# A two-layer graph attention network on one core: layer 2's destination factors as broadcast rows on ScalarE, and a new place and pace for layer 1's early pairs

## The chip, the core and the metric

The kernel runs on one core of a Trainium2 chip. The metric is the device time of one execution in microseconds; below a run means one execution. The core has five engines with a queue of instructions each: TensorE (PE, with its weight loads as PEld), VectorE (DVE), ScalarE (ACT), GpSimd (POOL) and SyncE (SP), and 16 DMA engines that move data between HBM and the on-chip memory. An engine takes its instructions in order: one that waits holds up all behind it.

## What is computed

6250 nodes with 768 features, 100,000 edges sorted by destination. The features are normalised and rectified, go through two layers of graph attention (four heads of 64 columns, then one head of 256), each followed by a relu, then through two dense layers, and the input is added. Cut to what matters here:

```python
def gat_conv(x, src, dst, W, a_src, a_dst, bias, heads):
    h = (x @ W).reshape(n, heads, -1)
    alpha_s = (h * a_src[None]).sum(-1)
    alpha_d = (h * a_dst[None]).sum(-1)
    e = jax.nn.leaky_relu(alpha_s[src] + alpha_d[dst], 0.2)
    e = jnp.exp(e - segment_max(e, dst)[dst])
    alpha = e / (segment_sum(e, dst)[dst] + 1e-16)
    return segment_sum(h[src] * alpha[:, :, None], dst).reshape(n, -1) + bias
h = jnp.maximum(_layernorm(x), 0.0)
h = relu(gat_conv(h, ..., W1, a_src1, a_dst1, b1, 4))     # layer 1
h = relu(gat_conv(h, ..., W2, a_src2, a_dst2, b2, 1))     # layer 2
return x + (relu(h @ Wm1 + bm1) @ Wm2 + bm2)
```

Every node also has an edge to itself. Numerator and denominator are summed together: a column of ones beside h makes the denominator. The weight of an edge is needed only up to a factor that depends on its destination, since that cancels. With s the source's score and d the destination's, exp(leaky_relu(s + d)) divided by exp(d) is max(exp(s), exp(0.2 s) * rho) with rho = exp(-0.8 d). So a source row carries e1 = exp(s) and e2 = exp(0.2 s), and only rho has to come from the destination. The same weight is exp(s + relu(-0.8 s - 0.8 d)).

## The kernel before

**Feature phase (to about 172 us).** For each of NT = 49 tiles of 128 nodes, x is loaded, normalised and multiplied by W1 (features1, L440); the row of a node, features and powers of its scores, stays on the chip (`kept`) and is stored to a table in HBM (store1, L473).

**Edges.** 782 edge tiles of 128 edges. Two tiles are a pair, four a group g (196 groups), eight a unit u (98), sixteen belong to one step of a node tile t, on average (49). For every edge tile GpSimd issues one indirect DMA (L645), which gathers the 128 source rows from the layer's table into half of a buffer G, one of 20 that hold a pair each. Gathers are issued AHEAD = 8 groups before their use. A buffer comes free when TensorE (and, in layer 1, VectorE) is done with its pair.

**rho to the edges.** For each unit a mask of 0 and 1 in bf16 (node by edge, 128x1024, make_mask L653, VectorE L662) is made in layer 1 and stored to `mask_d` (L664); layer 2 loads it back (fetch_mask L612). meet(t) (L683) multiplies each edge tile's mask with a narrow matrix `win` that holds rho in three bf16 parts: 16 matmuls for a node tile, 12 columns in layer 1 and 3 in layer 2 (L691). join(t) (L694) adds the three parts. `win` is built by prepare (L557), once for each layer.

**A pair (L703).** VectorE makes v = e2 * rho (L712) and w = max(v, e1) (L722 in layer 1, L715 in layer 2). Layer 1 then multiplies the gathered rows by w (L724), and TensorE sums them into the unit's 128 destinations with a one-hot matrix `hot` (L673) as weights. In layer 2 VectorE makes a one-hot matrix that is scaled by w (two L719 for a pair), which is TensorE's weights, and the gathered rows go through as they are. Both are L736 (o_ps), two matmuls and two weight loads for a tile.

**Node steps.** take_sum (L747) adds a unit's sum to the running one (VectorE L753) and copies finished quarters out (ScalarE L762). In layer 1, Node1.steps (L945) divides, transposes, multiplies by W2 and stores the row of table 2 (L966 and after). In layer 2, Node2.steps (L1055): divide (o, L1066), transpose (L912), relu with bias (rT, L918), first dense layer (L1075, then mT by L1080), second (y, bias L1024 and L1085), add x (L1089), store. The tables STEPS_AT and UP_AT give the half-groups at which the steps of a node tile are put into the queues of layer 2.

**Early tiles.** The first gathers of a layer would wait for its whole table. Eleven edge tiles of layer 2 are gathered while its last rows are missing, and the missing rows are added by one-hot matmuls (first_rows L322, first_whole L294). Layer 1 does so for 23 *early pairs* (SOON), which lie eight groups apart from group 11 on. They are gathered in the feature phase from as much of the table as is there (soon_rows L346), stored to `soon_d` in HBM (soon_away L356), loaded back into a buffer when their turn comes (soon_back L362), and completed: soon_sources loads their source numbers, soon_hits (VectorE L379) makes one-hot matrices for the node tiles that were missing, soon_missing (TensorE L389, 1028 matmuls in all) fetches the rows from `kept`, and soon_whole (VectorE L396) adds them. soon_away stores a pair as soon as the table is SOON_HELD = 6 tiles past the pair's stage, and all that are left at the start of layer 1.

**Order.** From L400 on the order on every engine is the order of the program. The loop over groups is:

```python
for g in range(NG):                       # t, j = divmod(g, 4)
    gather(g + AHEAD)
    pair(g, 0)
    advance(g); gather_up(...); make_hot(g + 1)
    if j == 0:   fetch_rows, soon_sources, prefetch(t), meet(t + 1), soon_hits(t)
    elif j == 2: ahead(t), soon_missing(t)
    elif j % 2:  soon_whole(t - 1) where j == 1; make_mask((g + 7) // 2)
    pair(g, 1)
    advance(g, 1)
    if j == 3: join(t + 1)
```

with the soon_ steps in layer 1 only (their number is the early tile k = 2 i + 0 or 1).

## Time and profile before

| | us |
|---|---|
| runs shown, median of 3 | 2571.82 (2562.27 to 2574.3) |
| the profiled execution, own time | 2580.24 |
| its span, first to last instruction | 2578.4 |
| gathers of layer 1 on GpSimd | about 172 to 1340 |
| GpSimd still, end of layer 1 | 1340.4 to 1375.8 |
| gathers of layer 2 | 1375.8 to 2527 |
| mean granted TensorE clock | 0.802 |

A matmul in single precision is two passes in the records, so a tile's L736 appears as two matmuls and two weight loads. The costliest groups of the page after the gathers, with line, engine, operation, operands and count, then busy time and mean duration in ns, and the idle time of the engine ahead of them with what ended most of it:

```profile
L736 PE MATMUL o_ps<-G,hw 128*128 128x258 f32 x1564 | 524.6, 463 | 225.5 <-issue 196.2
L736 PE MATMUL o_ps<-hw,hot 128*128 128x260 f32 x1564 | 504.6, 463 | 207.6 <-issue 128.8
...
L719 DVE TENSOR_SCALAR hw<-iota_ps,dcol,w 128x128 f32<-128x128 f32 x782 | 285.0, 406 | 15.4 <-DVE w L715 0.6
L724 DVE TENSOR_TENSOR hw<-G,e_ps 128x520 f32<-128x520 f32 x391 | 271.8, 695 | 22.5 <-DVE e_ps L722 6.3
L389 PE MATMUL missing<-kept,soon_hit 128*128 128x268 f32 x1028 | 251.4, 398 | 35.2 <-issue 35.2
L379 DVE TENSOR_TENSOR soon_hit<-soon_of,iota_ps 128x1408 f32<-128x1408 int32 (+18 forms) x46 | 75.6, 1643 | 323.2 <-remote 258.8
...
L691 PE MATMUL e_ps<-win,mask 128*128 128x12 bf16 (+1 forms) x1564 | 72.0, 168 | 130.9 <-issue 122.6
```

"issue" is time in which the engine waited for nothing that the profile shows, "remote" a releaser that it could not name. The page's 40 slices show the DMA engines full in the first three (351, 358 and 329 GB/s of the feature phase) and about half busy after. Idle time of an engine that is not the limit costs nothing.

### The profile page before, as it was taken

What the parts mean: (1) busy time and instruction counts of PE and PEld (TensorE: products, weight loads), DVE (VectorE), ACT (ScalarE), POOL (GpSimd) and SP (SyncE); (2) the same over time, 40 slices, a digit from 0 to 9 for tenths busy, and PEclk for the clock granted to TensorE, in tenths of its full rate; (3) what the DMA queues carried; (4) which work ended last, traced back from release to release, by engine and by line L of the source; (5) the groups of instructions that cost most, each with busy time, mean ns of one, the idle gap of its engine ahead of it and who ended that gap; (6) DMA issues with size and microseconds to landing.
All of it is one profiled execution on the core that took longest, in us unless ns stands there. A gap on an engine that the chain in (4) does not pass through costs nothing.

```text
span 2578.4 us, 26497 instructions
## 1 busy us (share of the span) xinstructions
PE 1809.2 (70%) x7727; PEld 1288.6 (50%) x7729; DVE 1397.1 (54%) x4195; ACT 409.4 (16%) x1273; POOL 1523.6 (59%) x1666
## 2 busy tenths in 40 slices
PE   9944768867767777677675656676766766777677
PEld 7732546646545555555553434454444444454455
DVE  7733666666666676576565443444444444444444
ACT  6730011111111111111111011111111111111111
POOL 5366555565655655565554566666666666666661
PEclk9975878878878888887888768777778778877778
DMA  9994444545544544454434434445554555444442
GB/s 351 358 329 114 143 140 137 147 137 147 149 141 143 154 143 143 143 149 138 142 107 125 126 113 152 146 140 152 153 150 136 151 152 156 151 136 145 148 147 76
DMA packets 167328, 400.37 MB, mean 155 GB/s; under 512 B 36631, under 2 KB 54254, under 8 KB 167174
## 3 DMA queue, kind: packets, MB, share of 16 engines
q0 software_dynamic: 75072, 211.10, 29.9%
q1 hardware_dynamic: 90732, 185.99, 21.0%
q10 hardware_dynamic: 1370, 1.48, 0.2%
q8 instruction: 65, 1.06, 0.2%
q14 instruction: 89, 0.73, 0.1%
HBM read 333.87 MB, written 64.56 MB: 155 GB/s over the span
## 4 chain that ended last, share of the span: by engine, by line
PE 30%; issue 22%; DVE 21%; another core or an unknown queue 16%; POOL 4%; DMA 3%; ACT 1%; SPq 0%; DVEq 0%; POOLq 0%; ACTq 0%
PE o_ps L736 17%; PE y_ps L1085 4%; DVE hw L724 4%; POOL G L645 4%; DVE hot L673 4%; PE missing L389 3%; PE h_ps L447 3%; DVE e_ps L722 2%; DVE e_ps L712 2%; DVE hw L719 2%; DMA G<-table,src_i 2%; DVE acc L753 2%; DVE mask L662 1%; PE tp L1075 1%
## 5 line engine op out<-in xcount | busy, mean ns | idle before, releaser
L645 POOL DMA_INDIRECT G<-table,src_i x1507 | 1431.5, 950 | 874.1 <-issue 377.3
L736 PE MATMUL o_ps<-G,hw 128*128 128x258 f32 x1564 | 524.6, 463 | 225.5 <-issue 196.2
L736 PE MATMUL o_ps<-hw,hot 128*128 128x260 f32 x1564 | 504.6, 463 | 207.6 <-issue 128.8
L736 PEld LDWEIGHTS o_ps<-G,hw 128*128 128x128 f32 x1564 | 353.0, 232 | 368.8 <-issue 272.0
L736 PEld LDWEIGHTS o_ps<-hw,hot 128*128 128x128 f32 x1564 | 337.8, 227 | 347.2 <-issue 169.0
L762 ACT ACTIVATE sum<-acc 32x260 f32<-32x260 f32 (+1 forms) x384 | 160.0, 417 | 1421.8 <-DVE hw L724 631.8
L719 DVE TENSOR_SCALAR hw<-iota_ps,dcol,w 128x128 f32<-128x128 f32 x782 | 285.0, 406 | 15.4 <-DVE w L715 0.6
L724 DVE TENSOR_TENSOR hw<-G,e_ps 128x520 f32<-128x520 f32 x391 | 271.8, 695 | 22.5 <-DVE e_ps L722 6.3
L389 PE MATMUL missing<-kept,soon_hit 128*128 128x268 f32 x1028 | 251.4, 398 | 35.2 <-issue 35.2
L379 DVE TENSOR_TENSOR soon_hit<-soon_of,iota_ps 128x1408 f32<-128x1408 int32 (+18 forms) x46 | 75.6, 1643 | 323.2 <-remote 258.8
L389 PEld LDWEIGHTS missing<-kept,soon_hit 128*128 128x128 f32 x1028 | 196.3, 195 | 75.2 <-issue 41.4
L1089 DVE TENSOR_TENSOR y<-y_ps,xt 128x384 f32<-128x384 f32 (+1 forms) x98 | 54.6, 557 | 289.8 <-PE o_ps L736 106.8
L1085 PE MATMUL y_ps<-wm,mT 128*128 128x384 f32 x392 | 182.0, 594 | 18.2 <-issue 15.5
L691 PE MATMUL e_ps<-win,mask 128*128 128x12 bf16 (+1 forms) x1564 | 72.0, 168 | 130.9 <-issue 122.6
L447 PE MATMUL h_ps<-w,r 128*128 128x264 f32 (+1 forms) x588 | 139.3, 390 | 9.6 <-ACT r L437 5.0
L691 PEld LDWEIGHTS <-mask 128*128 128x128 bf16 x1564 | 65.0, 100 | 148.0 <-issue 140.3
L673 DVE TENSOR_TENSOR hot<-iota_ps,dcol 128x512 f32<-128x512 f32 x196 | 133.6, 682 | 2.3 <-remote 2.3
L712 DVE TENSOR_TENSOR e_ps<-G,e_ps 128x8 f32<-128x8 f32 (+1 forms) x782 | 125.5, 160 | 5.2 <-issue 0.9
L1085 PEld LDWEIGHTS y_ps<-wm,mT 128*128 128x128 f32 x392 | 77.4, 219 | 98.4 <-issue 65.5
L447 PEld LDWEIGHTS h_ps<-w,r 128*128 128x128 f32 x588 | 108.8, 192 | 32.6 <-issue 7.2
L1080 ACT ACTIVATE mT<-tp,bm1c 128x128 f32<-128x128 f32 x98 | 30.6, 363 | 507.8 <-remote 235.1
L753 DVE SCALAR_TENSOR_TENSOR acc<-acc,keep,o_ps 128x260 f32<-128x260 f32 (+1 forms) x192 | 91.6, 477 | 14.3 <-PE o_ps L736 10.2
(415 smaller groups left out, 1246.8 us busy)
## 6 DMA issues: line engine op xcount, KB each, us to landing
xt<-in_x SPq DMA_DIRECT2D x96, 384.0 KB
drow<-dmod_d SPq DMA_DIRECT2D x49, 512.0 KB
mask_d<-mask SPq DMA_DIRECT2D x97, 256.0 KB
mask<-mask_d SPq DMA_DIRECT2D x97, 256.0 KB
G<-table,src_i POOLq DMA_INDIRECT x1507
xTt<-in_xT SPq DMA_DIRECT2D x49, 384.0 KB
out<-y SPq DMA_DIRECT2D x48, 384.0 KB
table<-kept SPq DMA_DIRECT2D x49, 134.0 KB
```

The lines of the kernel that those rows point to most:

```text
L389: nc.tensor.matmul(soon_p[k], hit[:, T - there], kept[T], start=(T == there), stop=(T == NT - 1))
L447: nc.tensor.matmul(h_ps[:, :n], r[:, k], w1[:, k, :n], start=(k == 0), stop=(k == KI - 1))
L645: nc.gpsimd.indirect_dma_start(out=G[k // 2][:, k % 2], out_offset=None, in_=table[layer], in_offset=bass.IndirectOffsetOnAxis(ap=src_i[:, ...
L673: nc.vector.tensor_tensor(hot[g][:, T[0]:T[0] + n], iota_ps.unsqueeze(1).to_broadcast([P, n, P]), dcol[:, k:k + n].unsqueeze(2).to_broadca ...
L691: nc.tensor.matmul(e_ps[t][:, at + k, :3 * H], m[:, k * P:(k + 1) * P], pre.win[:, 2 * u + 2], start=True, stop=True)
L712: nc.vector.tensor_mul(v, e2, rho)
L719: nc.vector.tensor_scalar(hw[:, t], iota_ps, dcol[:, k:k + 1], w[:, t], ALU.is_equal, ALU.mult)
L724: nc.vector.tensor_mul(hw, Gp[:, :, :RW[1]].rearrange("p t (h c) -> p t h c", h=H), w.unsqueeze(3).to_broadcast([P, 2, H, C + 1]))
L736: nc.tensor.matmul(o_ps[u], l, r[:, :RW[layer]], start=(g % 2 == 0 and k == 0), stop=(g % 2 == 1 and k == tiles(g)[-1]))
L753: nc.vector.scalar_tensor_tensor(acc, run[0], keep[:, u % 2:u % 2 + 1], o_ps.pop(u), ALU.mult, ALU.add)
L762: nc.scalar.activation(done[t][r], acc[r], AF.Copy)
L1085: nc.tensor.matmul(y_ps, mT[:, j], wm2[:, j, s * half:(s + 1) * half], start=False, stop=(j == KH - 1))
```

## The change

1. **Layer 2's weights.** Table 2's row now holds s and -0.8 s, no powers. slopes() takes -0.8 d of the nodes, spreads it by ScalarE copies into the order of the units (column 1 of sd[2], by quarters of 32 nodes), transposes it on TensorE, and stores it to `slope_d`: units 0 to 55 at group 150 of layer 1, the rest at the start of layer 2. fetch_slopes(k) loads the rows of eight units, broadcast to all partitions (512 KB), 13 times in layer 2. For a pair ScalarE computes twice relu(row + (-0.8 s)) and twice exp(that + s), 128x128 each, and VectorE multiplies each by the one-hot matrix (two scalar_tensor_tensor). In layer 2 there is no meet, no join, no L712 and L715, no mask; the mask stores of layer 1 go too.
2. **Early pairs.** soon_away(held) stores the oldest early pairs while more than `held` are in buffers. SOON_HELD is 16. By the order of the program 7 of the 23 stores are in the feature phase (18 before), and 16 at the start of layer 1 (5 before).
3. **Completion.** An early pair i whose group is G = 8 i + 11 has its sources loaded at group G - 13; tile 2 i has hits at G - 10, matmuls at G - 8, additions at G - 6; tile 2 i + 1 at G - 6, G - 5 and G - 3. Before, the sources came at G - 15, and the steps at G - 11, G - 9, G - 6, and at G - 7, G - 5, G - 2.
4. The space for GpSimd's DMA descriptors is halved (dynamic_dma_scratch_size).

```diff
                          10)]
-SOON_AT = {2 * (8 * i + 11) + 1: i for i in range(len(SOON))}
-SOON_FROM, SOON_HELD = min(SOON), 6
+SOON_GROUP = [8 * i + 11 for i in range(len(SOON))]
+SOON_AT = {2 * g + 1: i for i, g in enumerate(SOON_GROUP)}
+SOON_FROM, SOON_HELD = min(SOON), 16
 BARE = 8
+SLOPES, SLOPES_AT = 56, 150
...
-    def soon_away(there):
-        for i in sorted(soon_G):
-            if SOON[i] <= there:
-                nc.sync.dma_start(soon_d[i], soon_G.pop(i).rearrange("p t c -> p (t c)"))
+    def soon_away(held):
+        for i in list(soon_G)[:max(len(soon_G) - held, 0)]:
+            nc.sync.dma_start(soon_d[i], soon_G.pop(i).rearrange("p t c -> p (t c)"))
...
-    mask_d = dram.tile([NU * P, 8 * P], BF16, name="mask_d")
+    slope_d = dram.tile([NU, P], F32, name="slope_d")
     edges_stack.enter_context(tc.manual_schedule())
...
                 soon_rows(i + 1)
-                soon_away(i + 1 - SOON_HELD)
+                soon_away(SOON_HELD)
             if i >= 10:
...
         nc.scalar.activation(rho, d, AF.Exp, scale=SLOPE - 1.0)
+        win = None
+        if layer == 1:
...
-    def fetch_mask(u):
-        if u < NU:
-            b = (min(8 * u + 8, LAST) - 8 * u) * P
-            mask[u] = maskp.tile([P, 8 * P], BF16, name="mask")
-            nc.sync.dma_start(mask[u][:, :b], mask_d[u * P:(u + 1) * P, :b])
+    def slopes(pool, a, b):
+        n = b - a
+        rr = pool.tile([P, n + 2], F32, name=f"slope{a}")
+        nc.vector.memset(rr, 0.0)
+        for q, first, past in ((0, 0, 1), (1, 0, 0), (2, 0, 0), (3, -1, 0)):
+            lo, hi = max(a // 2 + first, 0), min(b // 2 + past, NT)
+            at = 2 * lo + (-1, 0, 0, 1)[q] - a + 1
+            r = slice(32 * q, 32 * q + 32)
+            nc.scalar.activation(rr[r, at:at + 2 * (hi - lo)].rearrange("p (n k) -> p n k", k=2),
+                                 sd[2][r, lo:hi, 1:2].to_broadcast([32, hi - lo, 2]), AF.Copy,
+                                 scale=SLOPE - 1.0)
+        p = ps.tile([P, P], F32, name="slope_ps", tag="e")
+        nc.tensor.transpose(p[:n], rr[:, 1:n + 1], ident)
+        turned = pool.tile([P, P], F32, name=f"slopeT{a}")
+        nc.scalar.activation(turned[:n], p[:n], AF.Copy)
+        nc.sync.dma_start(slope_d[a:b], turned[:n])
...
                 tc.tile_pool(name=f"sm{layer}", bufs=4) as sm:
-            G, hot, e_ps, o_ps = {}, {}, {}, {}
+            G, hot, e_ps, o_ps, slope = {}, {}, {}, {}, {}
+            def fetch_slopes(k):
+                if layer == 2 and k * 8 < NU:
+                    n = min(8, NU - 8 * k) * P
+                    slope[k] = eg.tile([P, 8 * P], F32, name="slope", bufs=2)
+                    nc.sync.dma_start(slope[k][:, :n], bcast(slope_d, n, k * 8 * P))
...
                 if layer == 2:
-                    return fetch_mask(u + 1)
+                    return
                 a, b = (t * P for t in both(u))
...
                                         ALU.is_equal)
-                nc.sync.dma_start(mask_d[u * P:(u + 1) * P, a:b], mask[u][:, a:b])
...
-                if t >= NT:
+                if t >= NT or layer == 2:
                     return
...
             def join(t):
-                if t >= NT:
+                if t >= NT or layer == 2:
                     return
...
                 Gp = G.pop(TPG // 2 * g + p)
-                e1, e2 = ((Gp[:, :, RW[1]:RW[1] + 4], Gp[:, :, RW[1] + 4:]) if layer == 1 else
-                          (Gp[:, :, HID:HID + 1], Gp[:, :, HID + 2:]))
-                at = TPG * (g % 4) + 2 * p
-                rho, v, w = (e_ps[g // 4][:, at:at + 2, k * H:(k + 1) * H] for k in range(3, 6))
-                nc.vector.tensor_mul(v, e2, rho)
                 if layer == 2:
-                    w = sm.tile([P, 2, H], F32, name="w")
-                    nc.vector.tensor_max(w, v, e1)
+                    u = g // 2
+                    rows = slope[u // 8][:, u % 8 * P:(u % 8 + 1) * P]
+                    w = sm.tile([P, 2, P], F32, name="w")
+                    for t in range(2):
+                        nc.scalar.activation(w[:, t], rows, AF.Relu, bias=Gp[:, t, HID + 2:])
+                    for t in range(2):
+                        nc.scalar.activation(w[:, t], w[:, t], AF.Exp, bias=Gp[:, t, HID:HID + 1])
                     hw = hwp.tile([P, 2, P], F32, name="hw")
...
                         k = TPG * g + 2 * p + t
-                        nc.vector.tensor_scalar(hw[:, t], iota_ps, dcol[:, k:k + 1], w[:, t],
-                                                ALU.is_equal, ALU.mult)
+                        nc.vector.scalar_tensor_tensor(hw[:, t], iota_ps, dcol[:, k:k + 1], w[:, t],
+                                                       ALU.is_equal, ALU.mult)
                 else:
+                    e1, e2 = Gp[:, :, RW[1]:RW[1] + 4], Gp[:, :, RW[1] + 4:]
+                    at = TPG * (g % 4) + 2 * p
+                    rho, v, w = (e_ps[g // 4][:, at:at + 2, k * H:(k + 1) * H] for k in range(3, 6))
+                    nc.vector.tensor_mul(v, e2, rho)
                     nc.vector.tensor_max(w, v, e1)
...
                 soon_sources(pre_pool, 0)
-                soon_away(NT)
+                soon_away(0)
                 fetch_rows(3)
...
                 gather(g)
+            fetch_slopes(0)
             matched()
...
                         fetch_rows(t + 4)
-                        if t % 2:
-                            soon_sources(pre_pool, (t + 1) // 2)
                     node.prefetch(t)
                     meet(t + 1)
-                    if layer == 1:
-                        soon_hits(pre_pool, t)
+                    if t % 4 == 1:
+                        fetch_slopes(t // 4 + 1)
                 elif j == (2 if t < NT - 1 else 1):
                     node.ahead(t)
-                    if layer == 1:
-                        soon_missing(t)
                 elif j % 2:
-                    if layer == 1 and j == 1:
-                        soon_whole(G, t - 1)
                     make_mask((g + 7) // 2)
+                if layer == 1:
+                    for i, at in enumerate(SOON_GROUP):
+                        for k, hits_at in ((2 * i, at - 10), (2 * i + 1, at - 6)):
+                            if g == hits_at + 3 + (k % 2 == 0):
+                                soon_whole(G, k)
+                            if g == hits_at:
+                                soon_hits(pre_pool, k)
+                            if g == hits_at + 1 + (k % 2 == 0):
+                                soon_missing(k)
+                        if g == at - 13:
+                            soon_sources(pre_pool, i)
                 if g == NG - 3:
...
                 hot.pop(g, None)
+                if layer == 1 and g == SLOPES_AT:
+                    slopes(pre_pool, 0, SLOPES)
                 if layer == 1 and g == NG - 6:
...
                 stay_warm(4)
-                for k in range(5):
-                    fetch_mask(k)
             while late:
...
                 row = kept[t][:, :TW[2]]
-                nc.scalar.activation(row[:, :HID], h_ps[:, :HID], AF.Copy)
-                powers(row[:, HID:HID + 1], row[:, HID + 2:], h_ps[:, HID:HID + 1])
+                nc.scalar.activation(row[:, :HID + 1], h_ps[:, :HID + 1], AF.Copy)
+                nc.scalar.activation(row[:, HID + 2:], h_ps[:, HID:HID + 1], AF.Copy, scale=SLOPE - 1.0)
                 nc.vector.memset(row[:, HID + 1:HID + 2], 1.0)
...
+            slopes(pre, SLOPES, NU)
             vars(pre2).update(vars(prepare(pre, 2, 1)))
...
     nc = bacc.Bacc("TRN2", target_bir_lowering=False, num_devices=1,
-                   dynamic_dma_scratch_size=8192)
+                   dynamic_dma_scratch_size=4096)
     args = [nc.dram_tensor(name, a.shape, mybir.dt.from_np(a.dtype), kind="ExternalInput").ap()
```

More of the change, by code (lines that the diff above doesn't have):

```diff
@@ L561, in prepare @@
         nc.scalar.activation(rho, d, AF.Exp, scale=SLOPE - 1.0)
-        parts = wk.tile([P, NT, H, 3], BF16, name="parts")
-        nc.vector.tensor_copy(parts[:, :, :, 0], rho)
-        r1 = wk.tile([P, NT, H], F32, name="r1")
-        nc.vector.tensor_sub(r1, rho, parts[:, :, :, 0])
-        nc.vector.tensor_copy(parts[:, :, :, 1], r1)
-        r2 = wk.tile([P, NT, H], F32, name="r2")
-        nc.vector.tensor_sub(r2, r1, parts[:, :, :, 1])
-        nc.vector.tensor_copy(parts[:, :, :, 2], r2)
-        win = wk.tile([P, NG + 4, 3 * H], BF16, name="win")
-        pv = parts.rearrange("p n h k -> p n (h k)").unsqueeze(2)
-        for q in range(4):
-            r = slice(32 * q, 32 * q + 32)
-            to = win[r, q:q + NG].rearrange("p (n j) k -> p n j k", j=4)
-            of = pv[r].to_broadcast([32, NT, 4, 3 * H])
-            if q % 2:
-                nc.scalar.activation(to, of, AF.Copy)
-            else:
-                nc.vector.tensor_copy(to, of)
-        nc.vector.memset(win[64:96, 0:2], 0.0)
-        nc.vector.memset(win[96:128, 0:3], 0.0)
-        nc.vector.memset(win[0:32, NG:NG + 4], 0.0)
+        win = None
+        if layer == 1:
+            parts = wk.tile([P, NT, H, 3], BF16, name="parts")
+            nc.vector.tensor_copy(parts[:, :, :, 0], rho)
+            r1 = wk.tile([P, NT, H], F32, name="r1")
+            nc.vector.tensor_sub(r1, rho, parts[:, :, :, 0])
+            nc.vector.tensor_copy(parts[:, :, :, 1], r1)
+            r2 = wk.tile([P, NT, H], F32, name="r2")
+            nc.vector.tensor_sub(r2, r1, parts[:, :, :, 1])
+            nc.vector.tensor_copy(parts[:, :, :, 2], r2)
+            win = wk.tile([P, NG + 4, 3 * H], BF16, name="win")
+            pv = parts.rearrange("p n h k -> p n (h k)").unsqueeze(2)
+            for q in range(4):
+                r = slice(32 * q, 32 * q + 32)
+                to = win[r, q:q + NG].rearrange("p (n j) k -> p n j k", j=4)
+                of = pv[r].to_broadcast([32, NT, 4, 3 * H])
+                if q % 2:
+                    nc.scalar.activation(to, of, AF.Copy)
+                else:
+                    nc.vector.tensor_copy(to, of)
+            nc.vector.memset(win[64:96, 0:2], 0.0)
+            nc.vector.memset(win[96:128, 0:3], 0.0)
+            nc.vector.memset(win[0:32, NG:NG + 4], 0.0)
         e1 = wk.tile([P, NT, H], F32, name="e1")
@@ L610, in fetch_rows @@
             nc.sync.dma_start(drow[r], bcast(dmod_d, 16 * P, r * 16 * P))
[L612 to L617 removed]
+    def slopes(pool, a, b):
[5 more added lines that the diff above has]
+            at = 2 * lo + (-1, 0, 0, 1)[q] - a + 1
+            r = slice(32 * q, 32 * q + 32)
+            nc.scalar.activation(rr[r, at:at + 2 * (hi - lo)].rearrange("p (n k) -> p n k", k=2),
[6 more added lines that the diff above has]
+        nc.sync.dma_start(slope_d[a:b], turned[:n])
     def layer_edges(layer, H, node, pre, matched, pre_pool):
```

## The prediction

> **What bounds the kernel now.** I read the page first, then the busy time by stretches, the groups by line between 1600 and 2200 us, and the timelines of GpSimd and TensorE over one stall. The page:
>
> ```profile
> PE 1809.2 (70%) x7727; PEld 1288.6 (50%) x7729; DVE 1397.1 (54%) x4195; ACT 409.4 (16%) x1273; POOL 1523.6 (59%) x1666
> ...
> L645 POOL DMA_INDIRECT G<-table,src_i x1507 | 1431.5, 950 | 874.1 <-issue 377.3
> ```
>
> No engine is full, so the rhythm has to be looked for in a stage. Layer 2's middle by stretches (length, then each engine's busy time and instruction count, granted clock, DMA share, GB/s):
>
> ```profile
> 1800.00:2000.00 200.00, 138.74 (x597) 95.05 (x597) 90.05 (x342) 28.83 (x76) 131.29 (x138) 0.77 0.49 146
> 2000.00:2200.00 200.00, 141.30 (x566) 91.58 (x566) 88.08 (x334) 29.39 (x77) 129.25 (x136) 0.77 0.50 149
> ```
>
> One gather is one line of the timeline, 0.95 busy and 0.30 of issue, 1.25 us in all. 1600 to 2200 holds 410 of them: 410 x 1.25 = 512 us. The other 88 us are pauses of GpSimd, and 410 gathers are 25.6 node tiles of 16, so 3.4 us of pause for each node tile. Here is a pause on GpSimd (start, length, line, idle before it), and TensorE over the same time:
>
> ```profile
> 1652.86 0.96 POOL L645 DMA_INDIRECT G<-table,src_i  x1 [0.30 <-issue]
> 1657.40 0.94 POOL L645 DMA_INDIRECT G<-table,src_i  x1 [3.59 <-remote]
> 1658.65 0.95 POOL L645 DMA_INDIRECT G<-table,src_i  x1 [0.30 <-issue]
> ```
> ```profile
> 1637.94 1.90 PE L736 MATMUL o_ps<-G,hw 128*128 128x258 f32 x8
> 1639.68 1.05 PE L1075 MATMUL tp<-rT,wm 128*128 128x128 f32 x8
> 1640.57 0.54 PE L691 MATMUL e_ps<-win,mask 128*128 128x3 bf16 x16
> 1640.97 0.69 PE L736 MATMUL o_ps<-G,hw 128*128 128x258 f32 x2
> ...
> 1644.17 0.38 PE L736 MATMUL o_ps<-G,hw 128*128 128x258 f32 x1 [1.06 <-issue]
> 1646.29 1.32 PE L736 MATMUL o_ps<-G,hw 128*128 128x258 f32 x2 [1.74 <-issue]
> ...
> 1656.84 0.59 PE L736 MATMUL o_ps<-G,hw 128*128 128x258 f32 x1 [0.81 <-issue]
> 1657.36 0.50 PE L1024 MATMUL y_ps<-bm2r,ones_r 3*128 3x384 bf16 x1
> 1657.79 2.93 PE L1085 MATMUL y_ps<-wm,mT 128*128 128x384 f32 x4
> ```
>
> To be seen: TensorE runs freely until 1641.6, then crawls for 15 us, an instruction per 0.7 us or a multiple of it, with waits that no data explains ("issue"); buffers of gathered rows fill, GpSimd pauses at 1653.8, and within 3 us TensorE is free again. GpSimd restarts and the cycle repeats, three pauses and three node tiles in about 70 us. The same pattern stands all through both layers, and never where GpSimd is idle (1344 to 1375) or before the gathers. Counted in the timeline, TensorE gets about 98 to 122 instructions through from the end of a long pause until it stalls, whatever the other engines do. So I read: while gathers run without a break TensorE has a quota of instructions, and a pause renews it. That is inferred, not shown. If so, the time of a layer is 1.25 us x gathers + pauses, and the pauses follow the number of TensorE's instructions.
>
> **What the Trainium skill says.** "ScalarE: Activation LUTs", What ACT_TABLE_LOAD costs: an activation with a bias pointer takes about 280 + 0.833 N ns, and neighbours overlap by about 93 ns. For 128 columns that is an estimated 387 ns; the trace has 363 (L1080), so I use 363 and about 0.28 for each in a row. "Runtime: NRT & Kernel Launch", Instruction fetch mechanics: each engine's instructions come through a FIFO filled in blocks of 256 by its own DMA queue. The page above has that traffic (q8, 65 packets, 1.06 MB); it fits a quota of instructions under heavy DMA, but 65 blocks in 2578 us are fewer than the stalls, so no run shows the link.
>
> **The change part by part**, against the profiled run of 2580.24 us (span 2578.4).
>
> *Layer 2, removed.* Per node tile 16 matmuls and 16 weight loads of L691, one join (L699, 0.2 us), and per pair L712 and L715 (157 + 160 ns) on VectorE; per unit one load of a 256 KB mask. Groups of 1600 to 2200: 812 matmuls of L736, 400 of L691, 204 of L1085, 200 of L1075, 51 of L1024, 50 of L912, each with its weight load, for 25.5 tiles: about 135 instructions a tile. 32 fewer is 24%. Pause per instruction is 3.4/135 = 0.025 us, so 0.8 us a tile; I take 0.73, as the semaphore instructions, which the groups leave out, would lie in the denominator too. Times 47 tiles in the steady part: **-34 us**. As pure matmul time (0.54 a tile) it would be hidden, since GpSimd's 20 us of gathers a tile exceed TensorE's 13 us of unstalled work. Bounds: 0 (pauses don't follow instructions) to -160 (47 x 3.4, all pauses gone).
>
> *Layer 2, added.* Per pair four 128x128 activations. ScalarE: 0.62 us for two in a row, 1.1 to 1.2 for four, at most 1.45 without overlap; 391 pairs make 430 to 570 us on some 165 there already in 1080: about 60% full, hidden on average. VectorE: two scalar_tensor_tensor in place of two L719 (406 ns). L753 takes 477 for 258 columns, and at about 1.04 ns a column 128 are 0.34 us, 0.41 at most; so VectorE falls from 1.04 to about 0.7 us a pair, which is cover, no gain. 13 loads of 512 KB replace 97 of 256 KB, no cost. What ScalarE's order does is the slower rival below; in the likeliest case 0, since the weights of a pair can be made as soon as its rows land, up to 14 hw buffers ahead.
>
> *Start of layer 2.* GpSimd stands 35 us before 1375.8 (layer 1's last tiles) and 15.5 before 1444, the second time with TensorE in the first tiles. Gone: the first 16 meets, the three-way split and spread of prepare (about 10 operations of VectorE, 2 of ScalarE), 5 mask loads. New: four copies, a transpose, a copy, a store and a broadcast load, some 5 us to landing, beside the gathers. **-3** (-5 to +5).
>
> *Layer 1.* The row's form (L966 one column wider, two small operations for the powers) and 97 mask stores off SP, none awaited: 0. Completion of early pairs: the same hits, matmuls and additions, an even pair one group later, an odd one one group later at the hits, its additions one earlier. What an addition at L396 waits for are matmuls two groups before it, as now; the largest waits of hits (L379, 258.8 us, "remote") are VectorE idling behind TensorE's stalls, not held up by the edit. 1028 matmuls remain. **0** (-15 to +10): stalls would only fall elsewhere.
>
> *Start of layer 1.* Seven stores of 268 KB leave SP in the feature phase in place of 18: 11 x 0.268 = 2.95 MB, 8 us at the 350 GB/s of the page's first slices, where DMA is the limit (share 0.98). They come back as 16 stores at layer 1's start in place of 5. GpSimd then finds 4 of 20 buffers free at once; stores of 0.8 us a pair run ahead of gathers at 2.5 us a pair. **-4** (-8 to +3).
>
> *End.* From the last gather (2527) to the end are about 20 pairs; ScalarE adds its part per pair at 1.1 us beside TensorE's 1.6: **+3** (0 to +8).
>
> *Scratch halved:* two or three gathers are in flight at once (1.25 us apart, landed in 2.4 to 2.9); cost 0, and if the ring were short every gather would lengthen, the one way it could be +100.
>
> Sum: -34 - 3 + 0 - 4 + 3 = -38, thus 2542 in a run like the profiled one. That lies 8 us above the median of the runs shown (2571.82), so the forecast is **2534 us**.
>
> **Rivals.**
> (a) *Pauses nearly vanish.* With 103 instructions a tile the quota of some 110 lasts one tile, 20 us of gathers, and the 20 buffers of pairs (50 us of gathers) could carry TensorE over. For: the margin is just there. Against: layer 1 pauses once a tile with as few. Gain 80 to 130 us: about 2465.
> (b) *The pauses belong to tiles, not instructions* (buffers against the burst of node steps). Then only the edges of the layer gain, -4 - 3 + 3, within 13 us of no change: about 2568. For it: the three pauses come with the three tiles of a cycle.
> (c) *Slower: ScalarE becomes a gate in order.* Now its waits cost nothing (page: mT waits 235.1 us "remote"). After, the weights of every pair stand behind rT, mT and sum (L762) in ScalarE's queue; these wait on TensorE's and VectorE's results, and TensorE waits for the weights behind them. After a stall TensorE would then have two or three pairs of hw ready and not eight, and run at ScalarE's 1.6 us a pair with node steps in it, not its own. It decides once ScalarE is late by more than the 0.73 us a tile that is gained; at an estimated 1.5 to 2.2 us a tile, a wait for one step, it is +70 to +105, less 34: about 2607. For it: queue order, and that ScalarE's added instructions may stall as TensorE's do. Against: 60% load and 14 buffers.
> (d) *The change doesn't do what it says.* "Kept in buffers" still stores and reloads all 23 early pairs; only the moment of 11 stores moves. I take that as so, and have priced it at -4.
>
> **How the numbers follow.** Forecast (2495 to 2558) 0.54; (a) 0.12; (b) 0.14; (c) 0.20. 0.5% (13 us) is about what a measurement can tell from no change. Faster: 0.54 + 0.12 = 0.66, same 0.14, slower 0.20. The range runs from (a) to (c)'s middle, 2460 to 2602; the likeliest case's own is 2495 to 2558.
>
> **What would show it.** The cycle in layer 2 falls from 70.4 to about 68 us for three tiles with fewer or shorter pauses, TensorE still getting 98 to 122 instructions between stalls; gathers stay at 1.25; ScalarE's added lines stand near 1.1 us a pair; the stretch from 172 to 1340 keeps its length. Wrong, if pauses are as long with a quarter fewer instructions (b), if TensorE or VectorE waits for L719's successor or for ScalarE's exponentials (c), or if GpSimd's pauses all but go (a).

## The result, and the profile after

Twenty runs of each kernel beside each other: 2575.26 us after, 2568.59 before, ratio of after to before 1.0026 with a 95% interval of 1.0014 to 1.0039. The forecast was 2534, faster. The change is a little slower: the 38 us did not come.

The profiled execution of the changed kernel took 2557.30 us, the shortest of its twenty (2557.3 to 2584.32); that of the kernel before took 2580.24, longer than all twenty timed beside it. So the two profiles stand 23 us apart the wrong way round, and what is read in them is shapes and rates, not totals. The page of the changed kernel (L666 is the gather, L739 VectorE's product for the one-hot matrix, L733 and L735 ScalarE's activations, L760 the sums):

```profile
PE 1718.3 (67%) x6948; PEld 1232.2 (48%) x6949; DVE 1239.2 (48%) x3356; ACT 865.5 (34%) x2796; POOL 1528.5 (60%) x1666
...
L666 POOL DMA_INDIRECT G<-table,src_i x1507 | 1436.4, 953 | 851.5 <-issue 382.8
L739 DVE SCALAR_TENSOR_TENSOR hw<-iota_ps,dcol,w 128x128 f32<-128x128 f32 x782 | 247.5, 349 | 549.7 <-ACT w L735 368.7
...
L733 ACT ACTIVATE w<-slope,G 128x128 f32<-128x128 f32 x782 | 267.1, 389 | 46.2 <-issue 32.8
L735 ACT ACTIVATE w<-w,G 128x128 f32<-128x128 f32 x782 | 267.7, 388 | 28.9 <-remote 15.8
```

The instructions are as many fewer as counted, the gathers cost what they did (953 ns, 950 before), ScalarE has its added work. GpSimd's idle time fell only from 874 to 852 us. The same two stretches of layer 2 that the prediction shows of before, now after:

```profile
1800.00:2000.00 200.00, 125.02 (x438) 83.68 (x438) 61.92 (x186) 106.55 (x345) 130.13 (x137) 0.81 0.44 128
2000.00:2200.00 200.00, 126.96 (x458) 87.88 (x457) 63.57 (x195) 112.82 (x363) 131.11 (x138) 0.79 0.46 133
```

TensorE has about a quarter fewer instructions (438 for 597, 458 for 566), and GpSimd gets through as many gathers as before (137 and 138 for 138 and 136). Over 1500 to 2300 us, a node tile's 16 gathers and their pauses take 23.24 us (23.39 before), 3.16 of it pause (3.28 before). Here is one such pause after, on GpSimd, and ScalarE and TensorE around it:

```profile
2042.72 0.95 POOL L666 DMA_INDIRECT G<-table,src_i  x1 [0.30 <-issue]
2047.29 0.95 POOL L666 DMA_INDIRECT G<-table,src_i  x1 [3.62 <-ACT mT L1111]
```
```profile
2034.17 0.68 ACT L735 ACTIVATE w<-w,G 128x128 f32<-128x128 f32 x2
2040.23 0.63 ACT L948 ACTIVATE rT<-tp,bT 128x128 f32<-128x128 f32 x2 [5.38 <-remote]
...
2043.73 0.40 ACT L735 ACTIVATE w<-w,G 128x128 f32<-128x128 f32 x1
2045.15 0.40 ACT L735 ACTIVATE w<-w,G 128x128 f32<-128x128 f32 x1 [1.02 <-ACT w L735]
2046.92 0.63 ACT L1111 ACTIVATE mT<-tp,bm1c 128x128 f32<-128x128 f32 x2 [1.37 <-remote]
```
```profile
2031.83 0.38 PE L942 MATMUL tp<-ident,o 128*128 128x128 f32 x2
...
2034.67 1.90 PE L760 MATMUL o_ps<-G,hw 128*128 128x258 f32 x8
2040.91 1.54 PE L1106 MATMUL tp<-rT,wm 128*128 128x128 f32 x8 [4.34 <-issue]
2042.24 2.01 PE L760 MATMUL o_ps<-G,hw 128*128 128x258 f32 x4
2047.53 2.95 PE L760 MATMUL o_ps<-G,hw 128*128 128x258 f32 x6 [3.27 <-DVE hw L739]
```

What to see: TensorE's transposes for rT ended at 2032.2, and ScalarE, free from 2034.9, starts rT at 2040.23. It waits for a completion that TensorE has had behind it for 8 us ("remote": a releaser that the profile cannot name, since it had long been done). mT goes the same way: it starts at 2046.92, 3.3 us after GpSimd's last gather ended (2043.67), and then GpSimd goes on. The crawl of one TensorE instruction per 0.7 us is gone, the pause isn't.

From the trace of each kernel I worked out how late mT starts: its start less the later of the end of TensorE's product for it and the end of ScalarE's instruction ahead of it. Median in layer 2: 5.9 us before (at most 17.0; 40 of 49 over 2 us, and 32 of these 40 start in a break of the gathers or within 0.3 us after one), 4.4 us after (31 of 49 over 2 us, 24 of these in a break).

### The profile page after: what moved, and what is told of

It reads as the page before. It is cut to its first block, busy times and chain, and to the rows that moved or that the text cites. A ratio compares the mean times of both kernels' runs of the same rounds, so it can differ in the third digit from the quotient of the medians.

```text
span 2555.5 us, 24791 instructions
## 1 busy us (share of the span) xinstructions
PE 1718.3 (67%) x6948; PEld 1232.2 (48%) x6949; DVE 1239.2 (48%) x3356; ACT 865.5 (34%) x2796; POOL 1528.5 (60%) x1666
## 5 line engine op out<-in xcount | busy, mean ns | idle before, releaser
L666 POOL DMA_INDIRECT G<-table,src_i x1507 | 1436.4, 953 | 851.5 <-issue 382.8
L760 PE MATMUL o_ps<-hw,hot 128*128 128x260 f32 x1564 | 496.5, 452 | 246.0 <-issue 159.7
L760 PE MATMUL o_ps<-G,hw 128*128 128x258 f32 x1564 | 465.8, 439 | 184.0 <-DVE hw L739 109.2
L739 DVE SCALAR_TENSOR_TENSOR hw<-iota_ps,dcol,w 128x128 f32<-128x128 f32 x782 | 247.5, 349 | 549.7 <-ACT w L735 368.7
L760 PEld LDWEIGHTS o_ps<-hw,hot 128*128 128x128 f32 x1564 | 331.9, 221 | 372.7 <-issue 213.1
L760 PEld LDWEIGHTS o_ps<-G,hw 128*128 128x128 f32 x1564 | 326.0, 220 | 309.1 <-DVE hw L739 138.0
L390 PE MATMUL missing<-kept,soon_hit 128*128 128x268 f32 x1028 | 266.1, 413 | 50.9 <-issue 50.6
L733 ACT ACTIVATE w<-slope,G 128x128 f32<-128x128 f32 x782 | 267.1, 389 | 46.2 <-issue 32.8
L735 ACT ACTIVATE w<-w,G 128x128 f32<-128x128 f32 x782 | 267.7, 388 | 28.9 <-remote 15.8
L390 PEld LDWEIGHTS missing<-kept,soon_hit 128*128 128x128 f32 x1028 | 207.4, 204 | 102.2 <-issue 63.4
L397 DVE SCALAR_TENSOR_TENSOR G<-G,soon_ok,missing 128x268 f32<-128x268 f32 x46 | 22.6, 492 | 187.0 <-remote 103.1
L1106 PE MATMUL tp<-rT,wm 128*128 128x128 f32 x392 | 59.6, 301 | 63.9 <-ACT rT L948 46.9
L746 DVE TENSOR_TENSOR e_ps<-e_ps,G 128x8 f32<-128x8 f32 x391 | 68.1, 174 | 53.4 <-remote 25.4
```

The source lines that it names most:

```text
L390: nc.tensor.matmul(soon_p[k], hit[:, T - there], kept[T], start=(T == there), stop=(T == NT - 1))
L666: nc.gpsimd.indirect_dma_start(out=G[k // 2][:, k % 2], out_offset=None, in_=table[layer], in_offset=bass.IndirectOffsetOnAxis(ap=src_i[:, ...
L733: nc.scalar.activation(w[:, t], rows, AF.Relu, bias=Gp[:, t, HID + 2:])
L735: nc.scalar.activation(w[:, t], w[:, t], AF.Exp, bias=Gp[:, t, HID:HID + 1])
L739: nc.vector.scalar_tensor_tensor(hw[:, t], iota_ps, dcol[:, k:k + 1], w[:, t], ALU.is_equal, ALU.mult)
L746: nc.vector.tensor_max(w, v, e1)
```

## The experiments

Three theories after the result, numbered as in the expectations. (1) *Meets and ScalarE cancel*: taking out the meets gave some 30 us, and ScalarE in the weights' path took them back. (2) *The halves cancel*: the early pairs' part gains some 15 us, layer 2's part loses 20. (3) *Pauses belong to tiles* (rival b): the meets gave nothing. Each run is timed beside the kernel before on the same chip. Four chips took part in the experiments, of two kinds: on the first kind the kernel before takes 2568 to 2590 us, as in all that is above, on the second 2100 to 2106. Sums of layer 2 below are from the first kind unless said otherwise. The ratio is the record's own; it isn't the quotient of the two medians beside it, and gains and costs below are worked out from it.

| run | median us | before, same call | ratio, 95% interval |
|---|---|---|---|
| the changed kernel (the result) | 2575.26 | 2568.59 | 1.0026 (1.0014 to 1.0039) |
| layer2_alone | 2584.25 | 2567.64 | 1.0069 (1.0044 to 1.0094) |
| early_alone | 2560.58 | 2567.64 | 0.9964 (0.9945 to 0.9983) |
| early_alone_again | 2580.77 | 2590.47 | 0.9966 (0.9951 to 0.9981) |
| no_meets | 2560.62 | 2567.64 | 0.9964 (0.9950 to 0.9978) |
| no_scalar_weights | 2554.51 | 2567.64 | 0.9958 (0.9941 to 0.9975) |
| tapered | 2574.99 | 2568.47 | 1.0019 (1.0004 to 1.0034) |
| tapered_wide | 2569.42 | 2568.47 | 1.0009 (0.9994 to 1.0024) |
| one_more_meet | 2581.08 | 2568.47 | 1.0044 (1.0018 to 1.0071) |
| *second kind:* changed_again | 2104.12 | 2105.84 | 0.9993 (0.9985 to 1.0002) |
| wide_steps | 2101.36 | 2100.12 | 1.0007 (1.0001 to 1.0014) |
| weights_ahead | 2110.59 | 2100.12 | 1.0049 (1.0035 to 1.0062) |
| ahead_and_wide | 2114.34 | 2100.12 | 1.0067 (1.0053 to 1.0080) |
| spaced_gathers | 2099.03 | 2100.12 | 0.9996 (0.9987 to 1.0004) |
| weights_ahead_again | 2112.80 | 2105.84 | 1.0040 (1.0026 to 1.0054) |
| wide_steps_again | 2107.45 | 2105.84 | 1.0008 (1.0000 to 1.0017) |
| scalar_unused | 2100.11 | 2104.77 | 0.9979 (0.9971 to 0.9987) |
| scalar_unused_again | 2096.29 | 2102.10 | 0.9970 (0.9958 to 0.9981) |
| scalar_no_rows | 2096.53 | 2104.77 | 0.9962 (0.9949 to 0.9976) |

### The change in two halves

layer2_alone is the changed kernel with the early pairs as before; early_alone is the kernel before with these lines of the change only:

```diff
-SOON_FROM, SOON_HELD = min(SOON), 6
+SOON_FROM, SOON_HELD = min(SOON), 16
...
-                        soon_hits(pre_pool, t)
...
+                            if g == hits_at:
+                                soon_hits(pre_pool, k)
...
-                   dynamic_dma_scratch_size=8192)
+                   dynamic_dma_scratch_size=4096)
```

> The kernel before with the change's layer 2 and nothing else (the descriptor space is halved, since layer 2's new rows need the room; early pairs are stored and completed as before). Theory 1 (the meets' removal gives about 30 us back, and ScalarE, which now stands in the weights' path and waits in order behind the node steps, takes it again): within 15 us of before, with VectorE waiting for ScalarE's L735 in layer 2. Theory 2 (the early pairs' parts gain some 15 us, and layer 2's part loses 20): 15 to 25 us slower than before. Theory 3 (pauses belong to node tiles, nothing in layer 2 matters): within 5 us of before.

> The kernel before with the early pairs kept, their completion spread anew and the descriptor space halved; layer 2 as before. Forecast on record: -4, within -23 to +13. Theory 2: -10 to -20 us. If the halved descriptor space cost anything, slower than before, with gathers above 1.25 us apart.

Layer 2's part costs 0.69%, 18 us; the early pairs' part gains 0.36%, 9 us; together +9, and the whole change measured +7. Theory 2 of the expectation has the signs. On another chip of the first kind the early part gained 0.34%:

> The early pairs' part alone, once more. Where completions come late: 4 to 14 us faster than before (ratio 0.9945 to 0.9983, as measured), the pause between the layers near 29 us. Where nothing comes late: within 4 us of before, since GpSimd then goes from layer 1 to layer 2 with a pause of some 3 us in any case.

That run fell where completions come late, so that the question whether the part gains elsewhere was not answered. One thing differs without scatter: GpSimd stands still between the layers for 35.0 to 35.4 us in three profiles without the early part (before, layer2_alone, no_meets), and for 27.9 to 28.2 in seven with it. But the last gather of layer 1 ends later there, at 1345 us in the mean against 1339, and the first gather of layer 2 is no earlier: 1375.8, 1369.4 and 1376.5 us without, and 1358.7, 1380.9, 1370.2, 1369.3, 1378.8, 1382.0 and 1374.5 with, mean 1374 and 1373. One execution of a kernel scatters by more than the gain, so whether these 7 us are the gain or are only shifted, the profiles don't tell. Gathers stayed at 1.25 us apart with half the descriptor space.

### The meets alone

```diff
                 if layer == 2:
+                    for u, _, _, _ in ranges(t):
+                        mask.pop(u)
+                    return
...
+                if layer == 2:
+                    rho, v = pre.rho[:, 0:2], sm.tile([P, 2, H], F32, name="v")
```

> The kernel before without layer 2's meets and joins: the destination's factor is left out of the weights (a constant column stands for it), VectorE's four operations for a pair, the masks' loads and all of layer 1 stay. It takes 32 of some 135 TensorE instructions from a node tile and adds nothing to ScalarE. Theory 1 and the forecast's reason (a pause for so many TensorE instructions): 25 to 40 us faster, 3.4 us of pause a tile falling to about 2.7. Theory 3 (pauses belong to tiles): within 8 us of before, still about 3.4 us of pause a tile.

9 us faster (6 to 13 by the interval), not 25 to 40. In its trace no stretch of layer 2 has TensorE at one instruction per 0.7 us or a multiple; before has about 50 such stretches, some 300 us together. The crawl went and all but 9 us of the time stayed, so in the main it was a symptom. GpSimd's pause in this one trace is 2.78 us a tile, near theory 1's 2.7; but single executions scatter, and early_alone and its repeat, with layer 2 as before, have 3.1 and 3.5. ScalarE, TensorE and GpSimd of no_meets around one pause (L1087 is mT, L1082 its product, L1092 the product that needs it):

```profile
2000.82 0.63 ACT L925 ACTIVATE rT<-tp,bT 128x128 f32<-128x128 f32 x2
2020.66 0.63 ACT L1087 ACTIVATE mT<-tp,bm1c 128x128 f32<-128x128 f32 x2 [19.22 <-remote]
```
```profile
2001.94 1.05 PE L1082 MATMUL tp<-rT,wm 128*128 128x128 f32 x8
...
2009.52 0.49 PE L1031 MATMUL y_ps<-bm2r,ones_r 3*128 3x384 bf16 x1
2021.08 2.93 PE L1092 MATMUL y_ps<-wm,mT 128*128 128x384 f32 x4 [11.07 <-ACT mT L1087]
```
```profile
2016.67 0.95 POOL L645 DMA_INDIRECT G<-table,src_i  x1 [0.30 <-issue]
2020.92 0.95 POOL L645 DMA_INDIRECT G<-table,src_i  x1 [3.30 <-remote]
```

The product ended at 2003.0; mT started 17.7 us later, 3 us after GpSimd had stopped for want of buffers. For 11 of these TensorE stood at the next product, which needs mT. TensorE runs out of work by waiting for its own completion to reach ScalarE, instead of crawling.

The reverse, the changed kernel with empty meets put back:

```diff
+                if layer == 2:
+                    extra = ps.tile([P, 16, 6], F32, name="extra", tag="e")
+                    for k in range(16):
+                        nc.tensor.matmul(extra[:, k, :3], idle[:, :P], idle[:, :3], start=True,
+                                         stop=True)
+                    return
```

> The changed kernel with 16 empty matmuls of 3 columns (and their 16 weight loads) for each node tile in layer 2, where the meets stood, nothing waiting for them. Where completions come late: 25 to 40 us slower than the changed kernel if a pause follows the number of TensorE's instructions, within 8 us if it follows the tile, with TensorE crawling at 0.7 us an instruction again. Where nothing comes late: within 3 us of the changed kernel, since they take 0.5 us a tile of TensorE's idle time.

1.0044 against 1.0026, 5 us with intervals that overlap. And the crawl is back, about 50 stretches and some 260 us of it. Its line for the stretch that above had 438 instructions of TensorE:

```profile
1800.00:2000.00 200.00, 137.84 (x590) 91.39 (x589) 61.67 (x185) 106.91 (x345) 130.17 (x139) 0.77 0.45 135
```

590 instructions in place of 438, and 139 gathers in place of 137. The number of TensorE's instructions does not set the pace, or only by the 5 to 9 us that these two runs leave to it.

### What ScalarE costs, and how

```diff
-                    w = sm.tile([P, 2, P], F32, name="w")
-                    for t in range(2):
-                        nc.scalar.activation(w[:, t], rows, AF.Relu, bias=Gp[:, t, HID + 2:])
-                    for t in range(2):
-                        nc.scalar.activation(w[:, t], w[:, t], AF.Exp, bias=Gp[:, t, HID:HID + 1])
...
-                        nc.vector.scalar_tensor_tensor(hw[:, t], iota_ps, dcol[:, k:k + 1], w[:, t],
-                                                       ALU.is_equal, ALU.mult)
+                        nc.vector.tensor_scalar(hw[:, t], iota_ps, dcol[:, k:k + 1],
+                                                Gp[:, t, HID:HID + 1], ALU.is_equal, ALU.mult)
```

> The changed kernel without ScalarE's four activations for a pair: VectorE scales the one-hot matrix by a column of the gathered row (weights left out), with two operations as before. TensorE's instructions as in the changed kernel. Theory 1: 30 to 50 us faster than the changed kernel, so 25 to 45 faster than before, VectorE no longer waiting for ScalarE. Theory 3: within 8 us of the changed kernel, so within 15 of before.

0.9958 against 1.0026: ScalarE's weights cost 0.68%, 17 us. A second, looser price comes from the halves: layer2_alone less no_meets is 1.05%, 27 us. This is the term that the forecast set at 0. If the reason was that weights stand in ScalarE's queue behind node steps that wait, putting them into the queue earlier must help; and if a tile's pause waits for mT, so must more room between the steps. `weigh_up_to` puts the weights six pairs ahead:

```diff
+                weigh_up_to(2 * g + p)
                 Gp = G.pop(TPG // 2 * g + p)
                 if layer == 2:
+                    hw = hws.pop((g, p))
...
-STEPS_AT = {t: [8 * t + 19 + k for k in (1, 2, 5, 8, 11, 14)] for t in range(NT - 2)}
+STEPS_AT = {t: [8 * t + 19 + k for k in (1, 2, 6, 12, 16, 20)] for t in range(NT - 2)}
```

(The second pair of lines is in tapered_wide only, which also moves the tile tp to the banks that the meets have left free.)

> The changed kernel with a pair's weights put into the queues of ScalarE and VectorE six pairs ahead, the lead falling to none over the last 24 pairs. On a chip where TensorE's completions come late: 10 to 25 us faster than the changed kernel if the weights' place in ScalarE's queue is what costs, within 8 us if not. On a chip where nothing comes late: within 5 us of the changed kernel, since the lead is gone at the end, where it cost 10 us before.

> The same with wide node steps and tp in the free banks. Where completions come late: a further 15 us or more if the hand-over from TensorE to ScalarE is what a pause waits for, nothing further if not. Where nothing comes late: within 6 us of the changed kernel.

tapered is where the changed kernel is (2574.99 and 2575.26). The queue's order did make TensorE wait: between 1600 and 2200 us it stood 47.6 us at o_ps for VectorE's product in the changed kernel, and next to nothing in tapered. But its wait for mT grew from 50.3 to 141.5 us over the same time, and nothing was gained: the place in the queue is not what costs. With wide steps mT is hardly late any more (over 2 us 9 times of 49, 45 us in sum; 38 times and 307 us in tapered), and 3 us are gained by the ratios, within what the intervals leave open. VectorE and TensorE of tapered_wide show where the waiting went (L1140 adds x to y, L1136 is the second dense layer's product):

```profile
2008.83 0.56 DVE L1140 TENSOR_TENSOR y<-y_ps,xt 128x384 f32<-128x384 f32 x1 [11.00 <-PE y_ps L1136]
2009.30 0.48 DVE L797 SCALAR_TENSOR_TENSOR acc<-acc,keep,o_ps 128x258 f32<-128x258 f32 x1
```
```profile
2002.39 0.80 PE L1136 MATMUL y_ps<-wm,mT 128*128 128x384 f32 x1 [2.48 <-issue]
2004.49 0.80 PE L1136 MATMUL y_ps<-wm,mT 128*128 128x384 f32 x1 [1.30 <-issue]
2006.58 0.80 PE L1136 MATMUL y_ps<-wm,mT 128*128 128x384 f32 x1 [1.30 <-issue]
```

The crawl is back, at the product of y, and VectorE stands 11 us at the addition. Take one late hand-over away and the next one takes its place; the pause is 3.03 us a tile.

What GpSimd itself stands for can be read in the kept traces. Besides instructions they hold the times at which completions are posted (the updates of the semaphores, the counters on which engines wait for each other). I count the pauses over 1 us of layer 2, from about the sixtieth gather on. In the kernel before there are 65, each ahead of the first gather into a buffer. In all 65 TensorE's last product from that buffer had ended before the pause began, a median 8.7 us before the gather (after: 50 of 51 pauses, 12.6 us). So GpSimd stood for the news of a free buffer, not for TensorE's work. 60 of the 65 pauses end with a burst of TensorE's completions, four or more within 0.3 us, which begins a median 2.3 us after the end of the last gather (after: 42 of 51, 2.7 us).

The same traces point to what ScalarE costs. From the burst to the next gather pass 0.30 to 0.34 us (medians) in the five traces in which ScalarE doesn't read the gathered rows (before, early_alone and its repeat, no_meets, no_scalar_weights), and 0.77 to 0.82 us in the five in which it does (after, layer2_alone, tapered, tapered_wide, one_more_meet). The profile's account of what ended GpSimd's waits between 1600 and 2200 us, before and then after (us in total, times, longest):

```profile
POOL G L645 <- PE o_ps L736: 44.3, 32, 3.6
POOL G L645 <- remote: 44.0, 23, 3.7
POOL G L645 <- PE y_ps L1024: 15.0, 6, 3.6
```
```profile
POOL G L666 <- ACT mT L1111: 46.2, 14, 4.6
POOL G L666 <- ACT w L735: 24.0, 38, 3.6
```

After, a buffer is free only when ScalarE, which takes its biases from the rows, is known to be done with it as well, and that news comes some 0.46 us later. 0.46 us for each of 51 pauses is an estimated 23 us, between the 17 and 27 above. The hand-over of the weights to VectorE is hardly late: between 1500 and 2450 us of the changed kernel VectorE's product starts over 1 us after its weights and VectorE itself are ready in 7 of 648 cases, at most 1.7. So the hold on the rows fits best; it is read from the traces, and no run on the first kind took the hold away alone.

### A chip without late completions

The first try at these questions fell on another chip:

> The changed kernel with ScalarE's activations and VectorE's products for a pair put into the queues three groups (six pairs) before TensorE uses them. If ScalarE costs its 20 us because the weights stand in its queue behind node steps that wait for TensorE (in-order gate), the changed kernel gets about 15 to 25 us faster, to the level of the one without ScalarE's weights, 2555. If ScalarE costs by its load alone, or by its reads holding the gathered buffers, within 8 us of the changed kernel or slower.

> The changed kernel with the node steps of layer 2 at half-groups 1, 2, 6, 12, 16, 20 after a tile's begin instead of 1, 2, 5, 8, 11, 14, and the tile tp in the two PSUM banks that the meets have left free. The first dense layer's product then has six pairs of time, not three, to be known to ScalarE. If the pause that each tile costs is the hand-over from TensorE to ScalarE (mT), which comes up to 17 us late while gathers run and stops TensorE at the next product, pauses fall below 2.5 us a tile and the kernel gets 20 to 60 us faster. If the pauses come from GpSimd learning late that buffers are free, or from the number of TensorE's instructions, within 10 us.

> The changed kernel with one tiny memset of GpSimd behind each gather of layer 2. If late completions of TensorE are a matter of gathers that run without a break, small breaks let them through: mT's start less late than 4 us in the median, pauses mostly gone, and the time the same or up to 50 us shorter. If only a break of some 3 us does, or none, longer by about the memsets' time, 771 times some 0.1 to 0.3 us.

> The changed kernel with both: weights three groups ahead and wide node steps. If the two gates are separate, the gains add: 35 to 80 us faster than the changed kernel. If one of them is the only gate, no more than the better of the two alone.

The kernel before took 2100 us there, 18% less, and nothing of the questions could be answered. So I ran the changed kernel itself:

> The changed kernel itself, beside the kernel before on whatever chip this is. Where TensorE's completions come late and GpSimd pauses (before at 2568): 0.26% slower as measured. Where they don't and GpSimd runs without a pause (before at 2100): GpSimd's gathers set the end in both kernels, so within 0.3%, with 1.25 us a gather, no pauses and less than 5 us between the layers.

0.9993, no change. It fell on a chip of the same kind. Two stretches of its layer 2:

```profile
1600.00:1800.00 200.00, 149.33 (x521) 97.67 (x520) 73.45 (x221) 133.09 (x412) 151.25 (x161) 0.83 0.52 151
1800.00:2000.00 200.00, 149.58 (x530) 97.39 (x528) 73.87 (x220) 133.49 (x414) 151.56 (x160) 0.85 0.52 150
```

160 gathers in 200 us are 1.25 us each: GpSimd never pauses, mT starts within 0.1 us in all 49 tiles, no two completions of TensorE in layer 2 are posted less than 0.2 us apart, and 2098.5 us of span are the feature phase, 1.25 us times the gathers, and 25 us of end. There the change moves nothing, because GpSimd covers it; ScalarE at 67% is covered too. weights_ahead costs 0.49% there, all at the end: 35 us from the last gather to the end in place of 25, which is why the lead in tapered falls to none. With wide steps it is 0.07%. spaced_gathers moved nothing: the gathers stayed 1.25 us apart, so the memsets made no break, and its question is open. weights_ahead and wide_steps repeated there gave 1.0040 and 1.0008.

The last question was whether ScalarE costs by its load and its hold on the gathered rows, or by handing each pair's weights to VectorE. In scalar_unused VectorE uses a column of the gathered row as in no_scalar_weights, and ScalarE still computes:

> The changed kernel with ScalarE's four activations for a pair computed and not used: VectorE scales the one-hot matrix by a column of the gathered row (weights left out). ScalarE's load, its reads of the gathered rows and so its part in GpSimd's waits stay; VectorE waits for ScalarE no more. Where completions come late: if the hand-over of the weights costs the 20 us, 15 to 25 us faster than the changed kernel (near 2555); if load or the hold on buffers does, within 8 us of it (2575). Where nothing comes late: within 4 us of the changed kernel.

In scalar_no_rows ScalarE's biases come from constants (the sources' scores are left out of the weights), so that it doesn't hold the rows:

> The changed kernel with ScalarE's four activations for a pair taking their biases from two constant columns, not from the gathered rows (the sources' scores are left out of the weights): same load, same hand-over to VectorE, but ScalarE neither waits for a gather nor holds its buffer. Where completions come late: if the hold on the gathered rows costs, 15 to 25 us faster than the changed kernel; if the hand-over or the load does, within 8 us. Where nothing comes late: within 4 us of the changed kernel.

Both fell on the second kind, scalar_unused twice (0.9979 and 0.9970; scalar_no_rows 0.9962). Against changed_again (0.9993, on the other chip of this kind) that is 0.1 to 0.3%, of which some 3 us lie in the end of the program (21 to 22 us after the start of the last gather in place of 25). Neither answers for the first kind: there the hold on the rows is what the traces point to, untried.

## Why the prediction was wrong

- *Layer 2, removed, -34 us: this step failed.* It read "a quota of TensorE's instructions that a pause renews" out of the crawl and priced a pause at 0.025 us an instruction. Taking out the 32 instructions gave 9 us (no_meets), putting them back cost 5 (one_more_meet): a quarter to a seventh of it. In its place stand pauses in which GpSimd waits for late news: buffers that TensorE had done with a median 8.7 us before (65 of 65 pauses), and completions that come in a burst after GpSimd has stopped. Whatever was changed in layer 2, GpSimd paused 2.8 to 3.6 us for 16 gathers (before 3.28, after 3.16, no_meets 2.78, tapered_wide 3.03, one_more_meet 3.57). Rival (b) fits that, as far as it says that the pauses don't follow the instructions; that they belong to the tiles is not shown (65 pauses over 1 us before, 51 after, for some 47 tiles), and no run changed the number of buffers or of gathers to a tile. That the lateness makes the pauses is read from traces: chips without the one have none of the other, but no run took the lateness away on a chip that has it. The steady count of 98 to 122 instructions between stalls was, it seems, only about a node tile's work, seen between two pauses. The profile had the warning: mT waits of 235 us for "remote", which the prediction put aside as a wait without a cost.
- *ScalarE added, 0: failed too.* It cost 17 to 27 us. Its reason was "hidden on average": that asks whether ScalarE has the time, not what its reading of the rows does to the buffers. In its place the traces show GpSimd waiting for ScalarE's completion too, some 0.46 us more a pause, an estimated 23 us; that this is the whole cost is not tried. The slower rival (c) named ScalarE, but by its order in the queue; tapered shows that the order is not the reason. Its figure has a slip besides: +70 to +105 less 34 is +36 to +71, or 2608 to 2643 from the median of 2572, so that 2607 is (c)'s lower end, and the range's upper end of 2602 is not its middle. The price of the instructions was right: four activations for a pair take 1.17 us in the timeline (two starts of L733 and two of L735 from 2040.75 to 2041.92), predicted 1.1 to 1.2. One takes 388 ns where the forecast took mT's 363; mT reads PSUM, the weights read SBUF, and the Trainium skill's figure ("ScalarE: Activation LUTs", What ACT_TABLE_LOAD costs), an estimated 387, agrees.
- *Early pairs, -4 at the start of layer 1:* -9, a little below its range of -8 to +3, and not at that place: the first gather of layer 1 starts at 172.0 to 180.2 us in three profiles without the part and at 169.2 to 180.0 in seven with it. GpSimd's stop between the layers is 7 us shorter; whether that is the gain is not shown. The respread of the completion and the kept buffers were not run apart.
- *End, +3:* 52 us from the start of the last gather to the end, before and after: 0. *VectorE's product:* 349 ns, predicted 340 to 410. *Scratch:* nothing, as said.
- *The sum:* -9 of the meets, -9 of the early pairs, +17 to +27 of ScalarE: -1 to +9, measured +7. The prediction's range held the time; its direction did not hold. The terms come from separate runs, and none shows that they add. The chance of 0.14 for (b) was too low: the view that spoke for it, three pauses for three tiles, was on the table.

The best version that leaves nothing out is early_alone, the early pairs' part without layer 2's: 0.35% faster than before on two chips of the first kind.

## What to carry to other kernels

When an engine crawls, ask whether it crawls because of its own work or because its results are not being taken: remove some of the work in a kernel of its own before pricing the crawl by the instruction. A wait for "remote", here a releaser long done, can be a late completion and belongs in the account of the critical path, even on an engine with hardly any load. Where the limiting engine pauses for a buffer, ask when the work on that buffer had ended: a buffer long free says that the news is late, not the work. And an engine that is 16% busy is no free place for work if it then reads a buffer that the limiting engine waits to have back: count whose completions must come in before the buffer is free.

## What the runs showed of the hardware

On the first kind of chip, while GpSimd issued gathers without a break, completions of TensorE came late: ScalarE saw one 17.7 us after the product's end in the example of no_meets, and mT started late by a median 5.9 us before and 4.4 after. 60 of 65 pauses (before) and 42 of 51 (after) end with a burst of four or more within 0.3 us, a median 2.3 and 2.7 us after the end of the last gather. Ahead of the burst in the pause shown above (after, 2043.67 to 2047.29) four postings of TensorE and ScalarE stand at 2044.43, 2045.13, 2045.84 and 2046.55: 0.70 to 0.71 us apart, the step of TensorE's crawl. In the changed kernel on the second kind mT's lag was within 0.1 us and no pause occurred.

The same program took 2104 us on one chip and 2575 on another, with the same 1.25 us for a gather on both and a granted clock of 0.88 against 0.80 in the profiled executions. What makes the difference between the chips no run shows. On the first kind the trace also lacks some postings (605 of TensorE for 754 instructions that post one, between 1500 and 2300 us of the changed kernel), on the second none (881 for 880 between 1200 and 2000 us of changed_again). Whether the recording of a profile has a part in the lateness was not tried, and stays a rival.
